# An attention and feed-forward layer in float32: LayerNorm outputs transposed whole, and split into high and low parts behind their transposing

## The chip, the cores and the metric

The kernel runs on one core of a Trainium2 chip. The metric is device time in microseconds (us) for one execution. Three runs of the kernel before took 1685.82, 1691.28 and 1694.91 us; the time before is their median, 1691.28 us.

The engines are called by their short names: PE is TensorE (matrix products and transposes, results in PSUM), PEld its weight loads, DVE is VectorE, ACT is ScalarE, POOL is GpSimd, and SP is the engine from whose queue all DMAs are issued here.

## The reference

`x` has 8 sequences of 1024 tokens with 256 features, in float32.

```python
x = x + layernorm(attn(layernorm(x), Wq, Wk, Wv, Wo))   # eps 1e-5, no weights
x = x + layernorm(ffn(layernorm(x), W, alpha, bias))

# attn: 16 query heads, 4 key/value heads, 16 features a head
q, k, v = x @ Wq, x @ Wk, x @ Wv
q, k = rope(q), rope(k)                     # pairs of neighbouring features
p = softmax(q @ k.T / sqrt(256))            # over all 1024 keys of the sequence
o = (p @ v) @ Wo

# ffn: weights of -1, 0 and 1
delta = 0.7 * mean(abs(W))
out = x @ (where(W > delta, 1, where(W < -delta, -1, 0)) * alpha).T + bias
```

## The kernel before

**Units and steps.** The work goes in 16 units of 512 query tokens (four tiles of 128); two units make a sequence. The inner work of a unit is cut into 32 steps, one for each pair of a head number j (0 to 3, taken for the four key/value heads r together) and a tile of 128 keys; there are 512 steps in all. In a step PE computes the scores with the keys on the partitions (four products, L624, each into a bank of PSUM called "se"), ACT takes their exps (L632, four of 128x512), and PE multiplies the exps of the step before with V (four products, L645, into a bank called "av"). The softmax needs each row's maximum ahead of the exp, so the scores are computed a second time with the queries on the partitions (L569, into pairs of banks called "sm"), DVE takes the maxima (L577), and this pass runs 11 steps ahead of the exps. The maxima of a block of eight steps are combined and split by DVE (L585, L590), transposed, copied by ACT (L598) and written by a DMA (`q_st<-mh`, L605) into two rows of the queries' operand. After the eighth key tile of a head ACT copies the product with V out of its bank (L658), and a DMA sends it to DRAM (`d_av<-avsb`, L666).

**High and low parts.** Products of float32 accuracy are made from operands of the type float32r, split into a high part of 12 significant bits and a low part, the rest. `split_hi` is a cast (L157 on POOL, L159 on ACT), and `split_lo` a subtraction (L162). `product` (L283) sums high by high, high by low and low by high, over two chunks of 128 features: six products for each output, or four where the right operand, the ternary weights, has no low part.

**Projections.** `Project` turns x of a unit into q, k and v. For each half of 256 tokens, `begin` computes LayerNorm's statistics on DVE and POOL (L237 to L243), the normed x on POOL (`xn`, L253), and its two parts on POOL (`xs`, L157 and L162). `x(p, l)` is `transposed` of half p and part l: four transposes of 128x128 against a float32r identity into one "se" bank (L267) and one cast by ACT (L271). Then come the products for k and v together (`kv`), for q (`q_product`), q's rotation on POOL (`rotate`, L297 to L299) and its split (tile `hlq`), and the writing of q and k to DRAM (`q_to_dram`, L471; `kt`, L429 and L480) and back, stacked (L541). The tiles `xs` and `hlq` share one buffer of the tag "hl", but for units 1 and 2, whose `xs` lie in buffers of the exps.

**Tails.** `Tail` is what follows a unit's attention. `fetch` reads the product with V and the softmax's denominators back from DRAM (L696, L701), `invert` and L713 spread the reciprocals, `scale` multiplies and splits on POOL (L719, L157, L162), `attn` is the product with Wo (tile `pa`), `stats_a` the LayerNorm and first sum, `stats_x` the statistics, the normed x and its split, `x(p, l)` the four transposes and the cast (tiles `pt_ot`, `ot`), `ffn` the product with the ternary weights (tile `pf`; L779 on ACT, L780 on POOL), and `stats_f` the last LayerNorm, the sum and the store (L790). The last unit has its own class, `LastTail`, which works by single tiles, transposes both parts at once (`o`), and uses DVE beside POOL.

**What sets the order.** The queues of PE, DVE and ACT are written out by hand over the whole kernel: each step lists its score products, and then the parts that are due in it. The parts' steps stand in tables, in steps from the start of the unit four before for projections (`P_PARTS`, L896), and from the start of the next unit for tails (`T_PARTS`, L907); so every middle unit's 32 steps carry one tail and, from two projections' tables, one projection. The first unit that goes this way has its own steps (`P_FIRST`), and so have the tail of unit 14 (`T_LAST`) and that of unit 15 (`L_PARTS`). Units 0 to 2 are projected in a prologue and ten first steps, -10 to -1, which are listed one by one (L934 to L960). POOL's queue is written by hand up to step 1 and again behind step 512. Between them the order on POOL, and on SP everywhere, is that of a scheduler which places each instruction in an idle place of its engine.

**Buffers.** The maxima use two pairs of banks, the exps' scores three banks, and the product with V one. Every part that needs PSUM takes one of the three "se" banks within its step:

```python
184        if spare[0]:
185            spare[0] += 1
186            if spare[0] % 5 < 2:
187                return ps_mx.tile(shape, dtype, tag="sm", name=name)
188        return ps_e.tile(shape, dtype, tag="se", name=name)
```

(`spare` is nonzero ahead of the first steps and behind the last only.) Work tiles such as `xt`, `ot` and the rotation's `t2` have two buffers each.

Of the kernel before, what the change touches and what calls it, by code (L numbers as in the profile page):

```python
# [28 lines left out]
def kernel(  # L29
# [39 lines left out]
    SPU = G * NK  # steps in a unit  # L69
    NSTEP = NU * SPU  # L70
    LEAD, START = 11, 10  # steps by which the maxima run ahead, and do so at the start
# [24 lines left out]
    # ---- constants and weights  # L96
# [35 lines left out]
    # Operands with parts that never change: rows of -1 in k, of 0 in q, columns of ones in v.  # L132
# [7 lines left out]
    def fill_rows(st, value, lo, n):  # L140
        """Rows lo .. lo + n of each half."""
# [22 lines left out]
    def split(eng, hi, lo, src, hi_eng=None):  # L164
        """src in two parts of 12 significant bits."""
        split_hi(hi_eng or eng, hi, src)
        split_lo(eng, lo, src, hi)

    # Weights in parts.  The columns of w_q go by their place in a pair.
# [9 lines left out]
    # A bank of PSUM for all that is not scores or their product with v.  Before and after those,  # L179
    # the banks of the maxima serve as well.  # L180
# [9 lines left out]
    # Ternary weights, transposed: wt[d, o] = (w[o, d] > delta) - (w[o, d] < -delta)  # L190
# [4 lines left out]
    def measure():  # L195
        ffn["ones"] = work.tile([P, P], F32, tag="qt", name="ones")
# [33 lines left out]
    # ---- layernorm over the last axis of [P, 2, D]  # L230
    def ln_stats(src):
        """(mean, -mean, 1 / sqrt(var + eps)) of each tile."""
# [29 lines left out]
    def transposed(src, tag, name, copy=nc.scalar.copy):  # L262
        """[P, 2, D] -> [P, ND, 2 * P], features on the partitions."""
# [10 lines left out]
    TERMS = ((0, 0), (0, 1), (1, 0))  # parts of the operands in a product  # L274
# [4 lines left out]
    def product(out, left, right, terms=TERMS):  # L279
        """The sum of left[i][:, c]^T right[j][:, c]."""  # L280
# [13 lines left out]
    def rotate(eng, x, cos, sin, t2):  # L294
        """x of [P, 2, n], the two of a pair on the same partition, in place."""
# [5 lines left out]
    # ---- projections of a unit: q and k rotated, transposed and split, v.  q comes out transposed,  # L301
    # with the two columns of a pair on the same partition.
    dq = {}

    class Project:
        """Its parts, each with at most one use of PSUM.  k's pairs are rotated with tokens on the
        partitions in the first units, and in the others by a way over DRAM."""

        def __init__(self, u, eng):
# [4 lines left out]
            if u not in (1, 2):  # L314
                xn = qkp.tile([P, UT, D], F32, tag="xn", name=f"xn_{u}", bufs=2)
                xs = qkp.tile([P, 2, UT, D], F32R, tag="hl", name=f"xs_{u}")
# [17 lines left out]
        def hi(self, p, eng=None):  # L334
            split_hi(eng or self.eng, self.xs[p][:, 0], self.xn[p])
# [692 lines left out]
    with tc.manual_schedule(engines={E.PE, E.DVE, E.Activation, E.Pool}):  # L1028
# [10 lines left out]
        for p in range(2):  # L1039
            p0.norm(p)  # L1040
            p0.hi(p)
# [114 lines left out]
```

## Time and profile before

| | |
|---|---|
| median of three runs | 1691.28 us |
| the profiled execution, its span | 1693.0 us |
| PE busy | 1572.8 us, 93%, 10200 instructions |
| PEld busy | 712.9 us, 42% |
| DVE busy | 1404.3 us, 83% |
| ACT busy | 1254.2 us, 74% |
| POOL busy | 834.1 us, 49% |
| DMA | 117.38 MB, 69 GB/s in the mean |
| granted clock of PE, mean | 0.988 |

The profile shows one execution; its own time is its span, 1693.0 us, which is 1.7 us above the median. Busy times of PE overlap, since its products are pipelined. Each line of the trace names the line of the code, the engine, the operation, and the tile that is written and those that are read, without their numbers: `ot<-pt_ot` is any copy of a transposed half of a tail. In a timeline the first figure is the start in us from the start of the span and the second the length; `x4` means four such instructions in a row, of which the length is the sum or stretch. A bracket such as `[0.69 <-PE sm L569]` tells how long the engine was idle before, and which instruction ended that. The order of the steps is seen from the products with V (L645): the distance from the first of one step to the first of the next is the length of a step.

### The profile page before, as it was taken

How to read it: one execution, taken by the hardware profiler on the slowest of the kernel's cores; microseconds unless marked ns; L12 is line 12 of the kernel's file. 1: busy time of each engine (PE TensorE's matmuls, PEld its weight loads, DVE VectorE, ACT ScalarE, POOL GpSimd, SP SyncE). 2: the span in 40 equal slices, each digit the busy share in tenths (PEclk: the TensorE clock that was granted, in tenths of full speed). 3: DMA queues.
4: the chain of work that ended last, by engine and by line, in shares of the span. 5: the costliest groups of instructions: out<-in, count | busy, mean ns of one | idle time of the engine just before them, and what ended most of it. 6: DMA issues, size and time to landing. Idle time of an engine off the chain costs nothing.

```text
span 1693.0 us, 27812 instructions
## 1 busy us (share of the span) xinstructions
PE 1572.8 (93%) x10200; PEld 712.9 (42%) x10200; DVE 1404.3 (83%) x1815; ACT 1254.2 (74%) x2457; POOL 834.1 (49%) x1239
## 2 busy tenths in 40 slices
PE   7989989999999999999999999999999999999998
PEld 5534343443434444443443434444443443333344
DVE  7877778888898888978888898888888888888884
ACT  4667767777777777777777777777777777777775
POOL 5543364473734637454473735637464362333354
PEclk8999999999999999999999999999999999999999
DMA  4341424134251412514133251412414132141100
GB/s 135 71 90 30 97 68 101 46 79 85 65 96 52 85 58 79 98 48 97 58 73 79 72 101 44 92 53 72 86 53 92 46 79 61 32 85 33 41 14 26
DMA packets 86040, 117.38 MB, mean 69 GB/s; under 512 B 12088, under 2 KB 50808, under 8 KB 85752
## 3 DMA queue, kind: packets, MB, share of 16 engines
q1 hardware_dynamic: 85904, 115.60, 29.7%
q8 instruction: 81, 1.33, 0.3%
q14 instruction: 55, 0.45, 0.1%
HBM read 68.65 MB, written 45.88 MB: 68 GB/s over the span
## 4 chain that ended last, share of the span: by engine, by line
PE 52%; DVE 18%; POOL 10%; ACT 10%; issue 6%; DMA 3%; SPq 1%; POOLq 0%; DVEq 0%; ACTq 0%
PE av L645 19%; PE se L624 17%; DVE mx L577 13%; ACT e L632 9%; PE sm L569 3%; PE pa L283 3%; PE pf L283 2%; PE pq L283 2%; PE pt_xt L267 2%; POOL hl L162 1%; PE pt_ot L267 1%; PE pkv L283 1%; DVE bnst L237 1%; DVE mhl L589 1%; POOL t L297 1%
## 5 line engine op out<-in xcount | busy, mean ns | idle before, releaser
L577 DVE TENSOR_REDUCE mx<-sm 128x2 f32<-128x1024 f32 x1024 | 1199.6, 1217 | 246.2 <-PE se L624 176.4
L632 ACT ACTIVATE e<-se 128x512 f32<-128x512 f32 x2004 | 1045.7, 605 | 315.0 <-PE sm L569 286.8
L624 PE MATMUL se<-q_st,k_st 64*128 64x512 f32 x2048 | 739.4, 445 | 77.7 <-ACT e L632 53.6
L569 PE MATMUL sm<-k_st,q_st 64*128 64x512 f32 x2048 | 758.3, 460 | 12.0 <-DVE mx L577 10.8
L624 PEld LDWEIGHTS se<-q_st,k_st 64*128 64x128 f32 x2048 | 338.5, 185 | 699.1 <-ACT e L632 432.6
L645 PE MATMUL av<-e,v_aug 128*32 128x512 f32 x4096 | 548.1, 606 | 0.0
L569 PEld LDWEIGHTS sm<-k_st,q_st 64*128 64x128 f32 x2048 | 327.2, 185 | 59.1 <-DVE mx L577 42.5
L241 POOL TENSOR_SCALAR lnsc<-mv 128x2 f32<-128x2 f32 (+1 forms) x134 | 26.1, 194 | 432.6 <-DVE mv L239 427.6
L645 PEld LDWEIGHTS av<-e,v_aug 128*32 128x32 f32 x4096 | 80.8, 108 | 87.7 <-issue 53.6
L780 POOL TENSOR_TENSOR a<-a,bias_bc 128x512 f32<-128x512 f32 x30 | 38.4, 1280 | 144.7 <-ACT a L779 144.7
L719 POOL TENSOR_TENSOR xn<-xn,a 128x512 f32<-128x512 f32 x30 | 38.4, 1280 | 122.7 <-DMA a<-d_rec 114.4
L242 POOL TENSOR_TENSOR lnsc<-lnsc,mhalf 128x2 f32<-128x2 f32 (+1 forms) x134 | 92.2, 688 | 0.9
L162 POOL TENSOR_TENSOR hl<-xn,hl 128x512 fp32r<-128x512 f32 x60 | 76.4, 1284 | 0.5
L253 POOL TENSOR_SCALAR xn<-x,lnsc 128x256 f32<-128x256 f32 x116 | 64.8, 566 | 3.5
L283 PE MATMUL pa<-woh,hl 128*128 128x256 f32 x240 | 47.3, 296 | 2.6 <-POOL hl L162 1.2
L237 DVE BATCH_NORM_STATS2 bnst<-a 128x6 f32<-128x256 f32 x120 | 44.5, 413 | 4.1 <-POOL a L780 4.1
L297 POOL TENSOR_TENSOR t<-q_rot,sin_q_sb 128x512 f32<-128x512 f32 x31 | 39.7, 1280 | 14.5 <-ACT q_rot L438 14.3
L283 PE MATMUL pq<-xt,wqkvh 128*128 128x256 f32 x256 | 45.9, 303 | 0.2 <-ACT e L632 0.2
L237 DVE BATCH_NORM_STATS2 bnst<-x 128x6 f32<-128x256 f32 x124 | 46.0, 413 | 0.2 <-DMA x<-in_L_attn_x 0.2
L271 ACT CAST xt<-pt_xt 128x512 fp32r<-128x512 f32 x64 | 39.1, 617 | 4.4 <-PE pt_xt L267 4.4
L271 ACT CAST ot<-pt_ot 128x512 fp32r<-128x512 f32 x66 | 40.7, 618 | 1.9 <-PE pt_ot L267 1.9
L162 POOL TENSOR_TENSOR hlq<-q_rot,hlq 128x512 fp32r<-128x512 f32 x31 | 39.7, 1282 | 4.7 <-ACT hlq L159 4.5
(155 smaller groups left out, 1273.9 us busy)
## 6 DMA issues: line engine op xcount, KB each, us to landing
q_st<-dq SPq DMA_DIRECT2D x90, 256.0 KB
dq<-hlq SPq DMA_DIRECT2D x60, 256.0 KB
d_av<-avsb SPq DMA_DIRECT2D x60, 256.0 KB
x<-in_L_attn_x SPq DMA_DIRECT2D x15, 512.0 KB
xn<-d_av SPq DMA_DIRECT2D x30, 256.0 KB
a<-d_rec SPq DMA_DIRECT2D x30, 256.0 KB
xr<-in_L_attn_x SPq DMA_DIRECT2D x15, 512.0 KB
out_x<-a SPq DMA_DIRECT2D x30, 256.0 KB
```

The costliest lines, as they stand in the source:

```text
L162: eng.tensor_tensor(lo, src, hi.bitcast(F32), ALU.subtract)
L237: nc.vector.bn_stats(st[:, t, :], src[:, t, :])
L242: nc.gpsimd.tensor_tensor(sc[:, 1, :], sc[:, 1, :], mhalf[:, :n], ALU.pow)
L253: eng.tensor_scalar(dst[:, t, :], src[:, t, :], sc[:, 0, t : t + 1] if eng is nc.gpsimd else mv[:, t, 0:1], sc[:, 1, t : t + 1], ALU.add i ...
L271: copy(dst, pt.bitcast(F32))
L283: nc.tensor.matmul(out, chunk(left[i], c), chunk(right[j], c), start=(k == 0), stop=(k == len(steps) - 1),)
L297: eng.tensor_tensor(dst, x, table.unsqueeze(1).to_broadcast(list(x.shape)), ALU.mult)
L569: nc.tensor.matmul(sc[:, a, :], queries[rows], ks[rows, r2, ch * 512 : (ch + 1) * 512], start=True, stop=True,)
L577: nc.vector.tensor_reduce(mx[i][:, ch, t, :, r2], sc, AX.X, ALU.max)
L624: nc.tensor.matmul(sc if len(queries.shape) == 2 else sc.rearrange("p (j t) -> p j t", j=G), ks[rows, r2, kt * P : (kt + 1) * P], queries[ ...
L632: nc.scalar.activation(e[:, a, :], sc, AF.Exp, scale=1.0 / D**0.5)
L645: nc.tensor.matmul(av_ps[0][32 * r : 32 * r + 32, :], va[:, kt, r, :], e[r // 2][:, r % 2, :], start=(kt == 0), stop=(kt == NK - 1),)
```

## The change

LayerNorm's output, which is the left operand of the projections and of ffn, was split into its two parts with tokens on the partitions, and each part was transposed. Now it is transposed once per half, in float32 against the float32 identity `ident`, and split behind that. The new function `transposed_split` does it in one of two ways. With `nc.vector`, ACT casts the high part out of PSUM and DVE subtracts it from the bank for the low part. With `nc.gpsimd`, ACT copies the whole bank to SBUF, into a tile of its own (tag "xt" or "ot", one buffer), and POOL casts and subtracts from there. The projections of units 2 to 15 and the tails of units 0 to 14 go the second way, the projections of units 0 and 1 the first (unit 0's engine is DVE, and unit 1 is given it). The tail of unit 15 stays as it was, with its split in a `stats_x` of its own.

`begin` and the tails' `stats_x` end with the normed x. The tiles `xs` are gone, so the tag "hl" of the projections holds `hlq` alone. `x` becomes one part per half where it was two. In `P_PARTS`, x of half 0 is at step 33 (33 and 34 before), that of half 1 at 43 (43 and 45). In `T_PARTS`, x of half 0 is at step 24 (24 and 25), that of half 1 at 28 (27 and 29). `P_FIRST`, `T_LAST`, the prologue and the first steps lose the same parts and are otherwise hardly moved. The tiles `t2` of q's rotation and those of the tag "qt" get one buffer where they had two. The diff also takes out comments and docstrings, by which lines behind L274 have other numbers; that is left out here.

```diff
@@ transposed() stays; behind it
+    def transposed_split(src, tag, name, lo_eng):
+        pt = psum([P, ND, 2 * P], f"pt_{name}")
+        for t in range(2):
+            for c in range(ND):
+                nc.tensor.transpose(
+                    pt[:, c, t * P : (t + 1) * P], src[:, t, c * P : (c + 1) * P], ident
+                )
+        hi, lo = (
+            work.tile([P, ND, 2 * P], F32R, tag=f"{tag}{l}", name=f"{name}_{l}") for l in range(2)
+        )
+        if lo_eng is nc.vector:
+            split_hi(nc.scalar, hi, pt)
+            split_lo(nc.vector, lo, pt, hi)
+        else:
+            whole = work.tile([P, ND, 2 * P], F32, tag=tag, name=name, bufs=1)
+            nc.scalar.copy(whole, pt)
+            split(lo_eng, hi, lo, whole)
+        return hi, lo
@@ class Project
-                xs = qkp.tile([P, 2, UT, D], F32R, tag="hl", name=f"xs_{u}")
-                self.xs = [xs[:, :, 2 * p : 2 * p + 2, :] for p in range(2)]
-                self.xs = [
-                    ep.tile([P, 2, 2, D], F32R, tag="e", name=f"xs_{u}_{p}") for p in range(2)
-                ]
-        def hi(self, p, eng=None):
-            split_hi(eng or self.eng, self.xs[p][:, 0], self.xn[p])
-        def lo(self, p, eng=None):
-            split_lo(eng or self.eng, self.xs[p][:, 1], self.xn[p], self.xs[p][:, 0])
         def begin(self, p):
             self.stats(p)
             self.norm(p)
-            self.hi(p)
-            self.lo(p)
-        def x(self, p, l):
-            self.xt[p, l] = transposed(self.xs[p][:, l], f"xt{l}", f"xt{l}_{self.u}_{p}")
+        def x(self, p, lo_eng=None):
+            self.xt[p, 0], self.xt[p, 1] = transposed_split(
+                self.xn[p], "xt", f"xt_{self.u}_{p}", lo_eng or self.eng
+            )
...
-            t2 = work.tile([P, 2, 2 * P], F32, tag="t2", name=f"t2_{self.u}_{p}")
+            t2 = work.tile([P, 2, 2 * P], F32, tag="t2", name=f"t2_{self.u}_{p}", bufs=1)
@@ class Tail
-        def x(self, p, l):
-            self.xt[p, l] = transposed(self.hl[p][:, l], f"ot{l}", f"ot{l}_{self.u}_{p}")
+        def x(self, p):
+            self.xt[p, 0], self.xt[p, 1] = transposed_split(
+                self.on[p], "ot", f"ot_{self.u}_{p}", nc.gpsimd
+            )
         def stats_x(self, p):
             self.sc[p] = ln_stats(self.x1[p])
             self.norm(p)
-            self.split(p)
@@ class LastTail
+        def stats_x(self, p):
+            super().stats_x(p)
+            self.split(p)
@@ the tables
     P_PARTS = (
-        (26, "begin", 0), (33, "x", 0, 0), (34, "x", 0, 1), (37, "begin", 1), (43, "x", 1, 0),
-        (45, "x", 1, 1), (49, "kv_and_dram"), (51, "q", 0), (52, "kt"), (53, "v"), (55, "q", 1),
+        (26, "begin", 0), (33, "x", 0), (37, "begin", 1), (43, "x", 1), (49, "kv_and_dram"), (51, "q", 0), (52, "kt"), (53, "v"), (55, "q", 1),
         (57, "q_to_dram"),
...
     T_PARTS = (
...
-        (23, "stats_x", 1), (24, "x", 0, 0), (25, "x", 0, 1), (26, "ffn", 0), (27, "x", 1, 0),
-        (29, "x", 1, 1), (31, "ffn", 1), (31, "stats_f", 0), (33, "stats_f", 1),
+        (23, "stats_x", 1), (24, "x", 0), (26, "ffn", 0), (28, "x", 1), (31, "ffn", 1), (31, "stats_f", 0), (33, "stats_f", 1),
...
-    P_FIRST = (47, 51, 52, 54, 57, 58, 59, 60, 62, 61, 63, 64)
-    T_LAST = (1, 3, 4, 5, 9, 10, 11, 14, 17, 20, 21, 21, 22, 24, 25, 26, 23, 27)
+    P_FIRST = (47, 51, 54, 57, 59, 60, 62, 61, 63, 64)
+    T_LAST = (1, 3, 4, 5, 9, 10, 11, 14, 17, 20, 21, 22, 24, 26, 23, 27)
@@ the first ten steps
-        [second("x", 1, 0), second("x", 1, 1), second("kv", 0)],
+        [second("x", 1, nc.vector), second("kv", 0)],
...
-        [second("q_product", 1), third("stats", 1), third("hi", 0, nc.scalar), third("lo", 0),
-         (pick, "q", 2, 0)],
-        [(pick, "q", 2, 1), third("norm", 1, nc.scalar), third("hi", 1, nc.scalar),
-         third("lo", 1), (keep_warm, 3), (fill_constant_parts, 1)],
-        [third("x", 0, 0), (pick, "q", 3, 0), (keep_warm, 3)],
-        [third("x", 0, 1), (pick, "q", 3, 1), second("rotate_q", 0), (keep_warm, 2)],
-        [third("x", 1, 0), third("x", 1, 1), second("split_q", 0)],
+        [second("q_product", 1), third("stats", 1), (pick, "q", 2, 0)],
+        [(pick, "q", 2, 1), third("norm", 1, nc.scalar), (keep_warm, 3), (fill_constant_parts, 1)],
+        [third("x", 0), (pick, "q", 3, 0), (keep_warm, 3)],
+        [(pick, "q", 3, 1), second("rotate_q", 0), (keep_warm, 2)],
+        [third("x", 1), second("split_q", 0)],
@@ the prologue
             p0.norm(p)
-            p0.hi(p)
-        for p in range(2):
-            p0.lo(p)
...
-        for p in x_parts:
-            part(projects, 0, *p)
+        for p in range(2):
+            p0.x(p)
...
-        p1.hi(0)
-        p1.lo(0)
...
-        p1.hi(1, nc.scalar)
...
-        p1.lo(1, nc.vector)
...
-        p1.x(0, 0)
-        p1.x(0, 1)
+        p1.x(0, nc.vector)
```

More of the change, by code (lines that the diff above doesn't have):

```diff
@@ L195, in measure @@
     def measure():
-        ffn["ones"] = work.tile([P, P], F32, tag="qt", name="ones")
+        ffn["ones"] = work.tile([P, P], F32, tag="qt", name="ones", bufs=1)
         nc.gpsimd.memset(ffn["ones"], 1.0)
@@ L828, in n @@
             if self.eng(t) is nc.gpsimd:
-                po = work.tile([P, G, HKV, 32], F32, tag="qt", name=f"pos_{self.u}_{t}")
+                po = work.tile([P, G, HKV, 32], F32, tag="qt", name=f"pos_{self.u}_{t}", bufs=1)
                 nc.scalar.copy(po, pt)
@@ L921, in keep_warm @@
             nc.tensor.matmul(warm[0], ident_r, sels[0][:, 0, 0], start=True, stop=True)
-    x_parts = [("x", p, l) for p in range(2) for l in range(2)]
     def pick(name, *args):
```

## The prediction

> **What bounds the kernel now.** I read the page first, then the groups by form, then the timeline of one unit of the middle (unit 7, about 785 to 886 us), since the averages mix stages.
>
> ```profile
> span 1693.0 us, 27812 instructions
> PE 1572.8 (93%) x10200; PEld 712.9 (42%) x10200; DVE 1404.3 (83%) x1815; ACT 1254.2 (74%) x2457; POOL 834.1 (49%) x1239
> ```
> TensorE (PE) looks like the bound, but its busy time overlaps itself. What decides is how long one of the 512 steps lasts. I read this off the timeline as the distance between the first L645 products of two steps. In unit 7: a step with no part 2.6 us, with only the copy of a finished block of attention (L658) 2.7, with one x part (four transposes into a score bank, one ACT copy) 3.2, with ffn 3.8, with attn, q or kv 4.3. These figures repeat within 0.1 in units 2 to 12, and such a unit lasts 101.1 us; units 13 and 14, which hold no projection, last 94. So a part costs what it adds to its step. This is why an x part costs 0.6 (timeline of PE and of ACT, step 27 of unit 7; columns: start, length):
>
> ```profile
> 868.78 0.50 PE L624 MATMUL se<-q_st,k_st 64*128 64x512 f32 x1
> ...
> 870.55 0.51 PE L267 MATMUL pt_ot<-ident_r,hl 128*128 128x128 f32 x4
> ...
> 871.99 0.50 PE L624 MATMUL se<-q_st,k_st 64*128 64x512 f32 x1
> ```
> ```profile
> 869.32 2.06 ACT L632 ACTIVATE e<-se 128x512 f32<-128x512 f32 x4 [0.69 <-PE sm L569]
> 871.25 0.62 ACT L271 CAST ot<-pt_ot 128x512 fp32r<-128x512 f32 x1
> 872.52 2.06 ACT L632 ACTIVATE e<-se 128x512 f32<-128x512 f32 x4 [0.66 <-PE sm L569]
> ```
> The next step's first score (871.99) starts when the copy has left its bank (871.87): four exps and one copy in series on ACT, not PE's work, set the step. In the chain of waits L283, L645 and L624 carry PE's 52%, and the list of waits has "se <- ACT ot" 47 times and "xt" 40 times at 0.8 us.
>
> **The change, part by part.** Steps are numbered within a unit; "x(p)" is the transposing of half p.
>
> *Half of the x parts go.* Each half had a high and a low part; it has one now. Of the 4 x parts that leave a middle unit, those of steps 2, 13, 25 and one of 27/29 go: 3.2 to 2.6, 3.1 to 2.6, 3.2 to 2.7 (L658 stays there), 3.2 to 2.6: -0.6 -0.5 -0.5 -0.6 = -2.2 us. Unit 13, without projections, shows the first two steps at 2.6 already.
>
> *The remaining transposes are float32.* L225 does four such:
>
> ```profile
> 136.37 0.66 PE L225 MATMUL pt_w<-ident,up 128*128 128x128 f32 x4 [0.25 <-ACT e L632]
> ```
> against 0.51 above, and the four of L823 take 0.60. So +0.09 to +0.15 an x part, but the transposes end about 0.2 us before ACT is free to copy (871.06 against 871.25), and a float32 copy out of PSUM takes 586 ns (L746) where the cast takes 618. I take 0 of bounds -0.03 and +0.12 for 56 parts (-2 to +7 us).
>
> The Trainium skill, FP8 and Floating Point Precision, TensorE Precision Notes, speaks against this: "True FP32: 4 passes through PE array". By it four transposes would take 4 x 0.51 = 2.0 us, 1.5 more for each of 56, and the kernel would be about 84 us slower. The L225 row has one matmul record to a transpose and 0.66 us, so I go by the row.
>
> *POOL's split moves behind the transposes.* It costs the same (hi 0.62, lo 1.28), but PE's products now wait for it. Three of the four have room: xt(0) at step 1 and xt(1) at 11 are read at 17, ot(1) at 28 is read at 31. ot(0) at 24 is read by ffn(0) at 26, and POOL's queue there is full (POOL's timeline, same unit):
>
> ```profile
> 858.50 1.27 POOL L297 TENSOR_TENSOR t<-q_rot,sin_q_sb 128x512 f32<-128x512 f32 x1
> ...
> 862.88 0.73 POOL L299 TENSOR_TENSOR q_rot<-q_rot,t 128x256 f32<-128x256 f32 x1
> 863.60 1.09 POOL L253 TENSOR_SCALAR xn<-x,lnsc 128x256 f32<-128x256 f32 x2
> ```
> In the built program POOL's order behind L299 is: ot(0) hi, xn(1), hlq hi, ot(0) lo, hlq lo. The rotation starts 0.1 earlier (POOL no longer splits before it, q_rot arrives at 858.31), so lo ends at 863.50 + 0.59 + 1.06 + 0.58 + 1.28 = 867.0. PE came to ffn(0) at 866.65; with step 25 shorter by 0.5 it comes at 866.1, does the two high products (0.25) and stands for 0.7 us. Queued behind it on PE: the rest of ffn, the step's L645, the next scores; DVE and ACT follow. So +0.7 in units 1 to 12, of bounds 0.3 (POOL slightly earlier) and 1.9 (POOL's whole queue to hlq lo).
>
> *attn(0) has no slack.* At step 12 it waits for POOL's scaled attention, which waits for a chain of DMAs begun at step 1. The sixth product of L283 starts 0.05 to 0.5 us after POOL's last lo in units 2 to 12 (0.28 in the mean; where the slack was used up, the 12 products span 2.1 to 2.4 instead of 1.67). Step 2 is 0.6 shorter and the chain is not: +0.3, of bounds 0 and 0.6.
>
> *A collision goes.* At step 28 POOL splits the next unit's xs while DVE splits the maxima:
>
> ```profile
> 875.18 0.59 DVE L585 TENSOR_TENSOR mc<-mx 128x16 f32<-128x16 f32 x1
> 875.80 0.18 DVE L589 CAST mhl<-mc 128x16 fp32r<-128x16 f32 x1
> 876.02 1.14 DVE L590 TENSOR_TENSOR mhl<-mc,mhl 128x16 fp32r<-128x16 f32 x1
> ```
> These two take 250 and 317 ns in the mean; here they end with POOL's L157 and L162. Step 30 then lasts 3.2 (2.8 in units 12 to 14, where no xs is split then). The split leaves step 28: -0.4. The one of xt(1) meets the maxima of step 12 instead, where DVE idles while PE does attn(0): 0, of bounds 0 and +0.4.
>
> The Trainium skill, SBUF — State Buffer, "SBUF: two separate sides", calls the port pair of the two engines an exclusive lock, held for the whole instruction, which the rows bear out.
>
> A middle unit: -2.2 + 0.7 + 0.3 - 0.4 = -1.6; eleven of them (2 to 12, less the 0.4 in 12): **-17.2 us**. Units 13 and 14 lose two x parts each with POOL idle: **-2.2**.
>
> *Start (to step 8 of unit 0).* Unit 0's low halves now stand on DVE behind the statistics of unit 1, whose x lands at 11.6; these end at 13.4, so PE's q product waits for 14.5 instead of starting at 12.3. Unit 1 saves transposes. The load of wo goes into the buffer of xn_2_1, read by transposes at step -1 (62 to 63) and no longer by POOL's split (55.0); POOL's L157 of wo stood at 68.2 waiting for it. SP's issues of dq, dk, k_st and then q_st<-mh (89.8) hang on POOL, and PE's step 8 on that. **+2**, of bounds 0.5 and 4.
>
> *Unit 1.* hlq_3 shared a buffer with xs_4, so POOL waited, and SP's queue, in which a q_st<-mh stands behind dq<-hlq, with it:
>
> ```profile
> 212.30 1.20 POOL L157 TENSOR_SCALAR hlq<-q_rot 128x512 fp32r<-128x512 f32 x2 [7.91 <-PE pt_xt L267]
> ```
> Steps 16 and 17 lasted 5.8 and 5.9 instead of 2.6 and 4.3: -4.8. But dq_3's four DMAs (1 MB) now go out at about 175.6, ahead of d_av:
>
> ```profile
> 173.26 2.31 SPq L541 DMA_DIRECT2D q_st<-dq  x5
> 175.67 0.38 SPq L666 DMA_DIRECT2D d_av<-avsb  x1
> ...
> 186.82 0.64 SPq L696 DMA_DIRECT2D xn<-d_av  x1
> 187.51 0.62 SPq L701 DMA_DIRECT2D den<-d_av  x1
> 188.23 1.42 SPq L605 DMA_DIRECT2D q_st<-mh  x2
> ```
> SP waits at L696 for d_av to land, and PE's step 8 (already 3.7 long through this) for the q_st<-mh behind. The queue moves 0.13 MB/us there, dq alone 0.16: +8 if all is added, +3.3 if the engines' spare half is used; I take **+5**. With three x parts of unit 0/1's own outside the stalls (steps 20 and 26 of unit 0, 13 of unit 1) and unit 1's steps 25 to 30 and ffn(0): -1.6 - 1.1 - 0.4 + 0.7 = -2.4. Unit 1 and the rest of unit 0: -4.8 + 5 - 2.4 = **-2.2**.
>
> *Unit 15.* x(0) at step 21 is read at 22 already. POOL's order is hi, xn(1), lo from 1643.9, so lo ends at 1646.9 where ffn(0) ended at 1645.8: +2, less 0.6 for the x part of step 25: **+1.4**, of 0 and 3.
>
> Sum: -17.2 - 2.2 + 2 - 2.2 + 1.4 = -18.2 us on the profiled span of 1693.0. That span lies 1.7 (0.1%) above the median of the three runs, 1691.28 (1685.82 to 1694.91); on the median it gives **1673 us**, 1.1% faster. A measurement tells this kernel from itself to about 0.5%, 8.5 us.
>
> **The rivals.** (1) *The wait at ffn(0) takes it all: slower.* Place: PE's L283 at step 26, behind POOL's ot lo. Each us is 12 us of the total, and it decides at 0.7 + 18.2 / 12 = 2.2 us: above this the change loses. It needs POOL 1.5 later than worked out; the L241 of the statistics, which stands between the sine and the cosine product, waits for DVE's mv (858.35, used at 859.85, 1.5 early), and that is what speaks against it. At a wait of 3.2: 1703. (2) *Little left.* The wait runs to 1.9 (+14.4) or the start and dq_3 take their upper bounds (+2, +3): 1688. For it: POOL has no gap from 854.85 to 868.36; against: its order is fixed and ot lo is not last. (3) *More gain.* The waits at ffn(0) and attn(0) vanish (-12) and dq_3's traffic is hidden (-5): 1656. Against: slack of 0.05 to 0.5 in ten units. (4) *Hidden anyway*, PE being 93% busy: 1691. Against it unit 13, whose steps 2 and 13 last 2.6.
>
> **How the numbers follow.** Forecast 0.64, its own range 1664 to 1682; (3) 0.12; (2) 0.11 and (4) 0.03, both within 0.5%; (1) 0.10. Faster 0.76, same 0.14, slower 0.10. The unknown costs add to -12 (attn 0.3 x 11, dq_3 1.7, ffn 0.4 x 12, start 1.5, end 1.4) and +18 (ffn 1.2 x 12, start 2, end 1.6): 1661 to 1691, which leaves out (1) and about half of (3).
>
> **What would show it.** Middle units of 99.5 us; steps 2, 13, 25, 27 at 2.6 or 2.7; a gap of about 0.7 within the eight products of L283 for pf(0) put down to POOL's lo; L283's pa(0) spanning 2.0 more often; step 30 at 2.8; unit 1's step 16 at 2.6 and its step 8 near 10. Wrong if x steps keep 3.2, if the float32 transposes outlast ACT's exps, or if PE waits over 2 us at ffn(0).

## The result, and the profile after

The changed kernel takes 1690.07 us (median of 12 runs, 1682.55 to 1694.36), the kernel before 1691.57 us in the 12 runs beside them. The ratio is 0.9992 with a 95% interval of 0.9977 to 1.0006: no difference that can be told, where 1.1% faster was forecast.

The first lines of the page of the changed kernel:

```profile
span 1689.4 us, 27228 instructions
PE 1564.0 (93%) x9952; PEld 697.7 (41%) x9952; DVE 1418.7 (84%) x1816; ACT 1223.6 (72%) x2390; POOL 832.8 (49%) x1239
```

PE has 248 instructions less and ACT 67, as the change says; DVE is busy 14 us longer with one instruction more: the three small instructions that combine and split the maxima (L594 to L599) take 73.7 us, where the same three (L585 to L590) took 58.2. The span is 3.6 us shorter than before. Line numbers have moved: the scores with keys on the partitions are L633, the exps L641, the product with V L654, the maxima L586, their split L594 to L599, the products of `product` L303, the new transposes L279, the whole copy L290.

Read as before, by the distance between the first products with V of two steps, the two profiles give where the time went (us; a negative figure is a gain):

| stretch | predicted | measured |
|---|---|---|
| start, to step 9 of unit 0 | +2 | +0.9 |
| rest of unit 0, and unit 1 | -2.2 | -1.8 |
| units 2 to 12 | -17.2 | -8.1 |
| units 13 and 14 | -2.2 | -1.0 |
| unit 15 | +1.4 | +6.4 |
| sum | -18.2 | -3.6 |

The steps of a middle unit, as means over units 2 to 12 (steps that differ by less than 0.05 are left out):

| step | 1 | 2 | 11 | 12 | 13 | 24 | 25 | 26 | 27 | 28 | 29 | 30 | 31 | unit |
|---|---|---|---|---|---|---|---|---|---|---|---|---|---|---|
| before | 3.19 | 3.19 | 3.19 | 4.50 | 3.13 | 3.19 | 3.19 | 3.80 | 3.20 | 2.61 | 3.19 | 3.22 | 3.81 | 101.16 |
| after | 3.25 | 2.61 | 3.32 | 4.75 | 2.61 | 3.35 | 2.65 | 4.33 | 2.61 | 3.25 | 2.60 | 3.48 | 3.87 | 100.43 |

Steps 2, 13, 25 and 27 lost what was forecast, 2.2 us together, and the part of step 29 is at 28 now. Step 26 holds the wait for POOL's low part. Its views, POOL's and PE's timeline of unit 7, and the same products on PE before the change:

```profile
853.09 1.28 POOL L317 TENSOR_TENSOR t<-q_rot,sin_q_sb 128x512 f32<-128x512 f32 x1 [1.61 <-ACT q_rot L447]
...
858.19 0.61 POOL L157 TENSOR_SCALAR ot<-ot 128x512 fp32r<-128x512 f32 x1
858.80 1.08 POOL L253 TENSOR_SCALAR xn<-x,lnsc 128x256 f32<-128x256 f32 x2
859.86 0.61 POOL L157 TENSOR_SCALAR hlq<-q_rot 128x512 fp32r<-128x512 f32 x1
860.44 1.27 POOL L162 TENSOR_TENSOR ot<-ot,ot 128x512 fp32r<-128x512 f32 x1
```
```profile
861.05 0.48 PE L303 MATMUL pf<-wt,ot 128*128 128x256 f32 x2
861.76 0.97 PE L303 MATMUL pf<-wt,ot 128*128 128x256 f32 x6 [0.24 <-POOL ot L162]
```
```profile
866.65 1.21 PE L283 MATMUL pf<-wt,ot 128*128 128x256 f32 x8
```

POOL's low part ends at 861.71, 8.62 us after its rotation starts; the sum in the prediction was 8.6. PE does the two high products and stands until then. The idle time is only 0.24 us, but the eight products stretch over 1.68 us where they took 1.21.

Step 30 was to fall from 3.2 to 2.8 and rose to 3.48. DVE's timeline of unit 7, and POOL's at the same time:

```profile
869.46 0.61 DVE L594 TENSOR_TENSOR mc<-mx 128x16 f32<-128x16 f32 x1
870.10 0.18 DVE L598 CAST mhl<-mc 128x16 fp32r<-128x16 f32 x1
870.32 1.15 DVE L599 TENSOR_TENSOR mhl<-mc,mhl 128x16 fp32r<-128x16 f32 x1
```
```profile
869.43 0.62 POOL L157 TENSOR_SCALAR ot<-ot 128x512 fp32r<-128x512 f32 x1 [2.15 <-ACT ot L290]
870.13 1.29 POOL L162 TENSOR_TENSOR ot<-ot,ot 128x512 fp32r<-128x512 f32 x1
```

DVE's two small instructions last 0.61 and 1.15 us and end with POOL's cast and subtraction, just as before. Only the tile on POOL is another: `ot`, the tail's second half, in place of `xs`. And units 13 and 14, where nothing was split at this place before, have step 30 at 3.48 too, where it was 2.84.

In unit 15 the tail of unit 14 has its first product with the ternary weights at step 22. PE's and POOL's timelines there:

```profile
1634.66 0.51 PE L303 MATMUL pf<-wt,ot 128*128 128x256 f32 x2
1637.13 0.97 PE L303 MATMUL pf<-wt,ot 128*128 128x256 f32 x6 [1.96 <-POOL ot L162]
```
```profile
1633.88 0.73 POOL L157 TENSOR_SCALAR ot<-ot 128x512 fp32r<-128x512 f32 x1
1634.60 1.25 POOL L253 TENSOR_SCALAR xn<-x,lnsc 128x256 f32<-128x256 f32 x2
1635.82 1.25 POOL L162 TENSOR_TENSOR ot<-ot,ot 128x512 fp32r<-128x512 f32 x1
...
1646.53 0.62 POOL L157 TENSOR_SCALAR ot<-ot 128x512 fp32r<-128x512 f32 x1
1647.23 0.19 POOL L241 TENSOR_SCALAR lnsc<-mv 128x1 f32<-128x1 f32 x1
1647.50 0.19 POOL L243 TENSOR_SCALAR lnsc<-mv 128x1 f32<-128x1 f32 x1
1647.65 1.28 POOL L162 TENSOR_TENSOR ot<-ot,ot 128x512 fp32r<-128x512 f32 x1
```

The first wait is 1.96 us, and steps 22 and 23 are 3.9 us longer together (6.25 and 3.91 for 3.34 and 2.87). Not all of this is the wait: behind it the granted clock was 0.50 from about 1638 to 1641.5. In the run below that moves the first product with the ternary weights in the other units, and leaves this tail as it is, the same wait was 1.97 us, the clock stayed at 1.00, and steps 22 and 23 took 5.78 and 2.85. The next products with V behind the wait, first of the changed kernel, then of that run with its wait:

```profile
1639.18 1.93 PE L654 MATMUL av<-e,v_aug 128*32 128x512 f32 x8
```
```profile
1631.59 0.97 PE L303 MATMUL pf<-wt,ot 128*128 128x256 f32 x6 [1.97 <-POOL ot L162]
...
1633.22 1.06 PE L654 MATMUL av<-e,v_aug 128*32 128x512 f32 x8
```

So the wait is worth 2.4 us here and the clock behind it 1.5. The second half's split stands at 1646.5 to 1648.9 between the statistics of the last tail (`128x1`), and steps 29 to 31 are 3.1 us longer together (11.8 for 8.7), with the clock at 0.50 from 1662.0 to 1668.8.

### The profile page after: what moved, and what is told of

Its sections match the earlier page's. It is cut to its first block, busy times and chain, and to the rows that moved or that the text cites. A ratio compares the mean times of both kernels' runs of the same rounds, so it can differ in the third digit from the quotient of the medians.

```text
span 1689.4 us, 27228 instructions
## 1 busy us (share of the span) xinstructions
PE 1564.0 (93%) x9952; PEld 697.7 (41%) x9952; DVE 1418.7 (84%) x1816; ACT 1223.6 (72%) x2390; POOL 832.8 (49%) x1239
## 4 chain that ended last, share of the span: by engine, by line
PE 53%; DVE 19%; ACT 10%; POOL 9%; DMA 5%; issue 3%; SPq 1%; POOLq 0%; DVEq 0%; ACTq 0%
PE av L654 20%; PE se L633 18%; DVE mx L586 14%; ACT e L641 10%; PE sm L578 4%; PE pq L303 3%; PE pa L303 3%; PE pf L303 2%; DMA a<-d_rec 1%; PE pkv L303 1%; DVE mhl L599 1%; DVE bnst L237 1%; POOL hl L162 1%; POOL q_rot L317 1%; POOL t L317 1%
## 5 line engine op out<-in xcount | busy, mean ns | idle before, releaser
L586 DVE TENSOR_REDUCE mx<-sm 128x2 f32<-128x1024 f32 x1024 | 1199.4, 1217 | 211.3 <-PE se L633 158.7
L641 ACT ACTIVATE e<-se 128x512 f32<-128x512 f32 x2004 | 1047.0, 603 | 322.9 <-PE sm L578 283.7
L633 PE MATMUL se<-q_st,k_st 64*128 64x512 f32 x2048 | 737.1, 444 | 78.0 <-ACT e L641 44.4
L578 PE MATMUL sm<-k_st,q_st 64*128 64x512 f32 x2048 | 759.1, 462 | 13.9 <-DVE mx L586 12.3
L633 PEld LDWEIGHTS se<-q_st,k_st 64*128 64x128 f32 x2048 | 337.5, 185 | 695.3 <-ACT e L641 460.6
L654 PE MATMUL av<-e,v_aug 128*32 128x512 f32 x4096 | 548.9, 608 | 0.1
L654 PEld LDWEIGHTS av<-e,v_aug 128*32 128x32 f32 x4096 | 81.1, 108 | 102.9 <-issue 70.6
L303 PE MATMUL pa<-woh,hl 128*128 128x256 f32 x240 | 47.8, 296 | 4.9 <-POOL hl L162 3.6
L303 PE MATMUL pq<-xt,wqkvh 128*128 128x256 f32 x256 | 46.0, 303 | 3.1 <-DVE xt L162 2.7
L303 PE MATMUL pf<-wt,ot 128*128 128x256 f32 x256 | 42.0, 298 | 6.8 <-POOL ot L162 4.6
L303 PEld LDWEIGHTS pq<-xt,wqkvh 128*128 128x128 f32 x256 | 36.2, 196 | 12.8 <-ACT e L641 8.8
L303 PEld LDWEIGHTS pa<-woh,hl 128*128 128x128 f32 x240 | 35.1, 189 | 15.1 <-POOL hl L162 5.8
```

Of the source, the lines that this page charges most:

```text
L303: nc.tensor.matmul(out, chunk(left[i], c), chunk(right[j], c), start=(k == 0), stop=(k == len(steps) - 1),)
L578: nc.tensor.matmul(sc[:, a, :], queries[rows], ks[rows, r2, ch * 512 : (ch + 1) * 512], start=True, stop=True,)
L586: nc.vector.tensor_reduce(mx[i][:, ch, t, :, r2], sc, AX.X, ALU.max)
L633: nc.tensor.matmul(sc if len(queries.shape) == 2 else sc.rearrange("p (j t) -> p j t", j=G), ks[rows, r2, kt * P : (kt + 1) * P], queries[ ...
L641: nc.scalar.activation(e[:, a, :], sc, AF.Exp, scale=1.0 / D**0.5)
L654: nc.tensor.matmul(av_ps[0][32 * r : 32 * r + 32, :], va[:, kt, r, :], e[r // 2][:, r % 2, :], start=(kt == 0), stop=(kt == NK - 1),)
```

## The experiments

All are edits of the changed kernel, but for the last. Where one profile alone was taken, its span stands against 1689.4 us of the changed kernel and 1693.0 us of the kernel before. The 12 runs of the changed kernel have spans of 1680.6 to 1692.3 us, so one span alone shows little, and the differences are read by steps; most repeat within 0.1 us from unit to unit, step 12 does not.

**The collision taken away, nothing moved.** The low part of the second half is left out, and the high part stands in its place.

```diff
         if lo_eng is nc.vector:
...
+        elif lo_eng is None:
+            split_hi(nc.scalar, hi, pt)
+            lo = hi
...
             self.xt[p, 0], self.xt[p, 1] = transposed_split(
-                self.on[p], "ot", f"ot_{self.u}_{p}", nc.gpsimd
+                self.on[p], "ot", f"ot_{self.u}_{p}", nc.gpsimd if p == 0 else None
             )
```

> Left out: the split of the second half of each tail's transposed LayerNorm output; ACT casts the high part straight out of PSUM and the product with the ternary weights uses it twice. PE and ACT have the same instructions in the same steps as in the changed kernel, only POOL's cast and subtraction behind step 28 are gone. Theory A (this split keeps POOL and DVE from each other while DVE splits the maxima): step 30 of units 2 to 14 falls from 3.48 to 2.84 us, DVE's subtraction L599 at step 29 from 1.15 to about 0.3, all other steps stay; 13 x 0.64 = 8.3 us less than the 1689.4 us of the changed kernel's profile, 1681. Theory B (step 30 is long because the transposes and the copy of step 28 push the maxima's products back): step 30 stays at 3.48, the time at 1689.

Step 30 was 2.83 in units 2 to 12, and 2.83 in 13 and 14; steps 28 and 29 stayed at 3.25 and 2.61. DVE's three small instructions took 0.18, 0.18 and 0.19 us in unit 7. The span is 1681.9, 7.5 us less. Theory A holds: with the same work on PE and ACT, the step's length hangs on POOL's split alone. Unit 15 falls from 99.7 to 96.3, all of it in steps 29 to 31 (8.4 for 11.8), so the split of the second half is also what lengthens the end.

**The second half's transposes one step later.**

```diff
-        (23, "stats_x", 1), (24, "x", 0), (26, "ffn", 0), (28, "x", 1), (31, "ffn", 1), (31, "stats_f", 0), (33, "stats_f", 1),
+        (23, "stats_x", 1), (24, "x", 0), (26, "ffn", 0), (29, "x", 1), (31, "ffn", 1), (31, "stats_f", 0), (33, "stats_f", 1),
```

> The changed kernel with one number changed: the second half's transposes of a tail at step 29 where they were at 28. Theory A (POOL's split meets DVE's split of the maxima at step 28 to 29): the split now comes behind it, step 28 goes from 3.25 to 2.6, step 29 from 2.6 to 3.25, step 30 from 3.48 to 2.84: 13 x 0.64 = 8.3 us less than the changed kernel, 0.5%. Theory B (it is the place of the transposes, not the split): the long step moves to step 31 and nothing is gained. A third way: the split now ends too late for the product with the ternary weights at step 31, which gives back up to 0.6 us a unit.

Steps 28, 29 and 30 were 2.61, 3.25 and 2.83, step 31 stayed at 3.87. The median is 1683.23 us, the ratio to the kernel before 0.9938 (0.9923 to 0.9953). DVE's timeline of unit 7 in this kernel:

```profile
867.37 0.18 DVE L594 TENSOR_TENSOR mc<-mx 128x16 f32<-128x16 f32 x1
867.58 0.18 DVE L598 CAST mhl<-mc 128x16 fp32r<-128x16 f32 x1
867.80 0.19 DVE L599 TENSOR_TENSOR mhl<-mc,mhl 128x16 fp32r<-128x16 f32 x1
```

The same three instructions end 0.62 us after the first began, against 2.01 us above. Theory A again, and the third way (too late for step 31) does not show.

**The first product with the ternary weights one step later.**

```diff
-        (23, "stats_x", 1), (24, "x", 0), (26, "ffn", 0), (28, "x", 1), (31, "ffn", 1), (31, "stats_f", 0), (33, "stats_f", 1),
+        (23, "stats_x", 1), (24, "x", 0), (27, "ffn", 0), (28, "x", 1), (31, "ffn", 1), (31, "stats_f", 0), (33, "stats_f", 1),
```

> The changed kernel with one number changed: the first product with the ternary weights of a tail at step 27 where it was at 26. If PE waits there for POOL's low part, the wait is gone: steps 26 and 27 together from 4.33 + 2.61 to 2.6 + 3.85, so 0.45 us a unit less in units 2 to 12 and nothing in 13 and 14: 1689.4 - 5 = 1684. The rival: POOL's addition of the bias behind this product (1.27 us) moves into the time in which DVE splits the maxima, and step 30 grows from 3.48 by up to 0.6, which takes it all: 1689 or more.

Steps 26 and 27 were 2.61 and 3.87, 0.46 less together; step 30 stayed at 3.48. The wait is gone and nothing took its place. The span is 1682.3; the wait explains 5 us of the 7, and unit 15, which the edit doesn't touch, was 1.8 shorter in this run, most of it behind the wait at step 22, where the clock stayed at 1.00.

**Only the projections' half of the change.** `Tail.x`, the tails' `stats_x` and the tails' steps are those of before.

> Only the projections' half of the change; the tails split and transpose as before, at the steps of before. If the tails' half costs what it gains and more: a middle unit of before (101.16) less 0.58 and 0.53 (steps 2 and 13), plus 0.18 (float32 transposes, steps 1 and 11), less 0.38 (no POOL split while DVE splits the maxima: step 30 from 3.22 to 2.84), plus 0.25 (attention's first product) = 100.1; units 13 to 15 as before (94.2, 94.2, 93.4); start and unit 1 as in the changed kernel (0.9 less). In all 1693.0 - 0.9 - 11 x 1.06 = 1680 on the profile, 0.75% faster than before. The rival, that both halves gain alike: half of the changed kernel's gain, 1691.

The median is 1685.14 us, the ratio 0.9942 (0.9924 to 0.9960). Middle units last 100.30 in the mean (100.1 was expected), with step 30 at 2.83; units 13 to 15 last 94.7, 93.9 and 93.3, as before. Half the change is faster than the whole, so the tails' half cost more than it gained. The profile's span, 1684.5, is 4.5 us above the expectation: step 8 of unit 1 took 13.7 us here, and step 12 of unit 2 took 6.4, both waits for DMAs.

**The tail of unit 14 split by ACT and DVE.**

```diff
             self.xt[p, 0], self.xt[p, 1] = transposed_split(
-                self.on[p], "ot", f"ot_{self.u}_{p}", nc.gpsimd
+                self.on[p], "ot", f"ot_{self.u}_{p}", nc.vector if self.u == NU - 2 else nc.gpsimd
             )
```

> The changed kernel, but the tail of unit 14, which runs in unit 15, splits the first way: ACT casts the high part out of PSUM and DVE subtracts from the bank. Theory A (unit 15 is longer because PE waits for POOL's low part at step 22, and because POOL's split of the second half stands ahead of the statistics of the last tail): steps 22 and 23 go from 6.25 and 3.91 to about 3.4 and 2.9, steps 29 to 31 from 11.8 together to about 8.7, and unit 15 from 99.7 to 93 to 94, as before the change. 1689.4 - 6 = 1683. Rival B (only the wait at step 22 is the split's doing): unit 15 at 96. Rival C: DVE, which has the last maxima until step 21 and half of the last tail, is the new bound, and unit 15 stays above 97.

Steps 22 and 23 were 3.3 and 2.9, steps 29 to 31 were 8.8 together, and unit 15 lasted 92.7, with a span of 1683.2: theory A. PE's timeline at step 22 has the eight products in one row:

```profile
1635.03 1.18 PE L303 MATMUL pf<-wt,ot 128*128 128x256 f32 x8
```

**Unit 3's queries to DRAM later, twice.** The first try moved one number of `P_FIRST`:

```diff
-    P_FIRST = (47, 51, 54, 57, 59, 60, 62, 61, 63, 64)
+    P_FIRST = (47, 51, 54, 57, 59, 60, 62, 61, 63, 74)
```

> The changed kernel with one number changed: unit 3's queries are written to DRAM ten steps later (step 10 of unit 1 where it was step 0). Theory A (this 1 MB of traffic ahead of the attention's output in SP's queue is what step 8 of unit 1 waits for): step 8 falls from 10.8 us to 3 or 4.9 at most, no other step grows, 6 to 8 us less: 1682. Rival B (step 8 waits for the attention's output for another reason): it stays at 10 to 11 and the time at 1689. Rival C: the traffic now hits the reciprocals' way over DRAM, and step 12 of unit 1 grows by as much as step 8 falls.

In the changed kernel the four DMAs of unit 3's queries (`dq<-hlq`) stand ahead of the sending of attention's output (`d_av`), of its reading (`xn<-d_av`) and of the maxima's rows (`q_st<-mh`), which step 8 waits for:

```profile
177.36 2.67 SPq L480 DMA_DIRECT2D dq<-hlq  x4
181.50 0.34 SPq L675 DMA_DIRECT2D d_av<-avsb  x1
...
193.03 0.64 SPq L705 DMA_DIRECT2D xn<-d_av  x1
...
194.44 1.41 SPq L614 DMA_DIRECT2D q_st<-mh  x2
```
```profile
197.87 0.76 PE L633 MATMUL se<-q_st,k_st 64*128 64x512 f32 x1 [7.60 <-DMA q_st<-mh]
```

With the edit, step 8 of unit 1 stayed at 10.5. This decided nothing, because the scheduler put two of the four DMAs at 178.8 us, still ahead of the reading of attention's output, and two ahead of the maxima's rows. So the second try moved what these DMAs read as well:

```diff
-    P_FIRST = (47, 51, 54, 57, 59, 60, 62, 61, 63, 64)
+    P_FIRST = (47, 51, 54, 57, 59, 60, 62, 61, 73, 74)
```

> The changed kernel with two numbers changed: unit 3's second half of q, and its queries' way to DRAM, at steps 9 and 10 of unit 1 where they were at the end of unit 0. In the run before this one (queries to DRAM ten steps later) half of that traffic still went out ahead of the attention's output and the other half ahead of the maxima, so it decided nothing; here all of it stands behind the maxima's rows that step 8 waits for, as before the change. Theory A (that traffic is what step 8 waits for): step 8 of unit 1 falls from 10.8 us to about 4.9, 5 to 6 us less than the changed kernel: 1684. Rival B (the wait has another cause in the start): it stays above 9, 1689. Rival C: the traffic hits the reciprocals' way over DRAM, and step 12 of unit 1 grows by as much.

Now step 8 is 7.2 and step 9 5.1. Step 9 holds 1.7 us of the product that came from step 31 of unit 0 (2.6 there for 4.3). So the two steps lose 14.0 - (12.3 - 1.7) = 3.3 us of the 5.0 that the change had added to them (8.9 before). The second of the two versions with all moves (below) has the same move, and there they lose 14.0 - (14.1 - 1.7) = 1.5. Without this 1.7 they take 10.6 and 12.4, less than in any run that leaves the traffic in its place (13.0 to 16.9). The last run, of the kernel before, shows it from the other side: its edit frees the buffer that unit 3's queries had to wait for, their four DMAs go out at 177.49, steps 16 and 17 of unit 1 fall to 2.6 and 4.3, and steps 8 and 9 take 13.3. So this traffic is a cause; its share is not settled by two executions that differ so. SP issues the maxima's rows at 187.43 here, and PE goes on with the next scores at 194.63, 7.2 us later (8.2 in that version); before the change it was 4.3 us (188.23 and 192.50). What else delays these 16 KB wasn't tried. SP's and PE's timeline of this run:

```profile
187.43 1.42 SPq L614 DMA_DIRECT2D q_st<-mh  x2
```
```profile
194.63 0.54 PE L633 MATMUL se<-q_st,k_st 64*128 64x512 f32 x1 [4.19 <-DMA q_st<-mh]
```

The span of this run is no shorter (1693.2), since step 12 lasted 5.7 in unit 8 and 7.9 in unit 9. That step is the next experiment.

**Attention's first product one step later.**

```diff
-        (1, "fetch"), (7, "invert"), (8, "scale", 0), (9, "scale", 1), (12, "attn", 0),
+        (1, "fetch"), (7, "invert"), (8, "scale", 0), (9, "scale", 1), (13, "attn", 0),
```

> The changed kernel with one number changed: attention's first product of a tail at step 13 for 12, a step that the change has emptied. Theory A (this product has no slack against the chain of DMAs and POOL's scaling that began at step 1): step 12 falls to 2.6 in every unit, step 13 is 4.35 in every unit, together 6.96 for 7.36 in the mean of units 2 to 12, and the single units with 5 us and more at step 12 are gone: 14 x 0.4 = 5.6 us less, 1684. Rival B (POOL is the later one and simply comes later still): step 13 is 4.8 in the mean and nothing is gained, 1689.

Step 12 is 2.61 and step 13 is 4.35, each within 0.1 in all of units 1 to 14; in the changed kernel step 12 ran from 4.3 to 5.4. Theory A; the span is 1681.2. This wait was 0.40 us a unit in the mean, of which the change had added 0.25 by these two profiles; the other runs with this product at step 12 have 4.6 to 5.0 there in the mean, where the kernel before has 4.5.

**The same transposes in float32r.** The tiles of the normed x get the type float32r as well.

```diff
-        pt = psum([P, ND, 2 * P], f"pt_{name}")
+        pt = psum([P, ND, 2 * P], f"pt_{name}", F32R)
...
-                    pt[:, c, t * P : (t + 1) * P], src[:, t, c * P : (c + 1) * P], ident
+                    pt[:, c, t * P : (t + 1) * P], src[:, t, c * P : (c + 1) * P], ident_r
```

> Left out: the low half of the normed x. It is written as float32r, so that the same transposes run in float32r against the float32r identity, as before the change; copy, cast and subtraction follow as in the changed kernel. Theory A (the float32 transposes cost 0.06 to 0.16 us a part): steps 1, 11, 24 and 28 of a middle unit go from 3.25, 3.32, 3.35 and 3.25 to 3.19 or below, 0.4 us a unit, 4.5 us in all: 1685. Rival B (the kind of the transposes is hidden behind ACT's exps, and these steps are longer for POOL's and ACT's order): they stay, 1689.

Steps 1, 11, 24 and 28 are 3.14, 3.19, 3.20 and 3.13, so 0.11 to 0.15 us less each, about 0.5 us a unit: the kind of the transposes is seen, theory A. But the time is not shorter: 1690.1, and a middle unit lasts 100.54. Step 26 is 0.18 longer than in the changed kernel and step 30 0.11, for PE comes earlier to waits whose end has not moved; step 12, which varies from run to run, has 0.25 more. Unit 15 shows what the clock did in the changed kernel: here it stayed at 1.00 through steps 29 to 31, and these took 9.1 us, 0.5 more than before the change. The groups by form, first of the changed kernel, then of this one (busy us, mean ns of one):

```profile
L279 PE MATMUL pt_xt<-ident,xn 128*128 128x128 f32 x128 | 21.7, 297 | 1.2
```
```profile
L279 PE MATMUL pt_xt<-ident_r,xn 128*128 128x128 f32 x128 | 17.3, 260 | 1.6 <-DVE xn L253 0.4
```

**The moves together**, first with the first of the two moves of unit 3's queries, then with the second:

> The changed kernel with five moves together: the second half's transposes of a tail at step 29 for 28, the first product with the ternary weights at 27 for 26, attention's first product at 13 for 12, unit 3's queries to DRAM ten steps later, and the tail of unit 14 split by ACT and DVE. If the causes are those named and do not overlap: 8.3 + 5 + 4 (step 12 from 4.75 to 2.6 and step 13 from 2.6 to 4.3, 14 units) + 7 + 6 = 30 us less than the changed kernel's profile, 1659 us, 2% faster than before. If they hide one another (the rival): 1675.

> The version with all moves, but with the move of unit 3's queries of the run beside it. If step 8 of unit 1 falls from 10.2 to 5: 1661 - 5 = 1656 on the profile, 2.1% faster than the kernel before. If rival B or C holds: 1661.

The medians are 1665.07 us, ratio 0.9829 (0.9811 to 0.9846), and 1662.07 us, ratio 0.9805 (0.9789 to 0.9821). Which of the two is faster isn't told by these. A middle unit lasts 98.9 and 99.0 us, and the units 2 to 12 differ by at most 0.6 where they differed by 1.2. The expected 1659 was nearly reached by the first (span 1660.9); the 7 us expected from its move of the queries did not come, as the run above says, and the other moves gave more than they were put down for (attention's, put down at 4, gives 14 x 0.4 = 5.6 by its own run). In the second, step 8 of unit 1 is 8.4 and not 5.

**The kernel before with two of the moves.** `attn(0)` at step 13, and the first half of `xs` in a buffer of its own; the tiles `t2` and those of the tag "qt" get one buffer, as in the change.

```diff
-        (1, "fetch"), (7, "invert"), (8, "scale", 0), (9, "scale", 1), (12, "attn", 0),
+        (1, "fetch"), (7, "invert"), (8, "scale", 0), (9, "scale", 1), (13, "attn", 0),
...
-                xs = qkp.tile([P, 2, UT, D], F32R, tag="hl", name=f"xs_{u}")
+                xs0 = qkp.tile([P, 2, 2, D], F32R, tag="xs0", name=f"xs0_{u}")
+                xs1 = qkp.tile([P, 2, UT, D], F32R, tag="hl", name=f"xs1_{u}")
...
-                self.xs = [xs[:, :, 2 * p : 2 * p + 2, :] for p in range(2)]
+                self.xs = [xs0, xs1[:, :, :2, :]]
```

> The kernel before the change, with the two moves that can be made in it too: attention's first product at step 13 for 12, and the first half of the parts to be transposed in a buffer of its own, so that POOL's split of it need not wait until the queries are written and comes ahead of DVE's split of the maxima (the rotation's tile gets one buffer to make room). If the collision and the reciprocals' way are causes in that kernel too: step 30 from 3.22 to 2.84, steps 12 and 13 from 7.63 to 6.95, a middle unit from 101.16 to 100.1, in all 13 us less: 1680 on the profile, 0.8% faster. Then what the change itself is worth is seen between this kernel and the version with all moves: about 20 us. If the moves help only the changed kernel: 1690.

The median is 1688.98 us, the ratio 0.9960 (0.9947 to 0.9974). Step 30 is 2.83, as expected: the collision cost the kernel before 0.39 us a unit. Steps 12 and 13 are 2.61 and 4.84, together 7.45 and not 6.95, because step 13 holds an x part in that kernel, so the product has no free step to go to. The change empties that step. With the waits moved away in both, a middle unit lasts 100.56 without the change and 99.0 with it.

## Why the prediction was right or wrong

**How the bound was read: right.** A part costs what it adds to its step. Steps 2, 13, 25 and 27 and the pair 28 and 29 gave -2.18 us a unit where -2.2 stood. The rival that PE's load hides it falls.

**The wait at the first product with the ternary weights: right.** +0.53 where +0.7 stood, and the move to step 27 took 0.46 of it away.

**Attention's first product: right.** +0.25 for +0.3, and the run that moves it shows that there was no slack. That the two agree so closely is in part luck, since the other runs give +0.1 to +0.5.

**"A collision goes. The split leaves step 28: -0.4": wrong, the largest error, and the step that failed.** The split of `xs` left, but the split of `ot(1)`, which the change moved behind its transposes, came to the same place. Its room was checked against its reader on PE (28 to 31), and not against what DVE does at that time. Measured +0.25 in the mean of units 2 to 12 and +0.64 in 13 and 14: 2.8 + 1.3 us lost where 4.0 were to be gained, 8.1 us of the 14.6 that are missing. Taking the split away and moving it both bring step 30 to 2.83.

**Float32 transposes, taken as 0: mis-sized.** The four take 0.66 us, as the row of L225 said, but the 0.15 more is not hidden: +0.06, +0.12 and +0.16 at steps 1, 11 and 24 and 0.06 at 28, 0.4 us a unit, between 4 and 5 us in all. The ground given, that the transposes end 0.2 us before ACT is free, was taken from one step, and the whole copies took 596 ns in the projections and 617 in the tails (medians), not 586. By the Trainium skill's four passes (FP8 and Floating Point Precision, TensorE Precision Notes) it would have been 1.5 us a part; these transposes do not show it.

**Unit 15, +1.4 of 0 to 3: mis-sized, +6.4.** The wait at step 22 was 1.96 us, as worked out (2). By itself it makes step 22 2.4 us longer and step 23 no longer, as three runs with the same tail and the clock at 1.00 show (5.8 and 2.9). The other 1.5 us there came with a granted clock of 0.50 behind the stall, which the prediction had at nothing. And the second half's split on POOL ahead of the last tail's statistics was not looked at: 3.1 us in steps 29 to 31, of which 0.5 are left in the run with float32r transposes, where the clock stayed at 1.00 there. Splitting by ACT and DVE took both away, 7.0 us. The 6.4 is the upper end: five other profiles with the same tail have unit 15 at 97.2 to 98.8 us, 3.9 to 5.4 more than before.

**The start and unit 1: right in size, in part by luck.** +0.9 for +2 and -1.8 for -2.2. Step 16 of unit 1 went to 2.6, step 8 to 10.8 ("near 10"). That unit 3's queries are a cause there is shown, but not how much of it they are. The start of one profile says little: the runs with the same start leave step 9 at 99.2 to 102.6 us, the kernel before at 100.0.

The median lies within the range of 1661 to 1691, but not in the forecast's own, 1664 to 1682, and no rival came true as it was told. The time is that of "little left", but the wait at the first product did not run to 1.9 us; two places that no rival named did it. Two slips in the working change nothing: the lower costs add to 12.7 and not 12, and the three lines said to carry PE's 52% of the chain carry 44.

## What to carry to other kernels

When an instruction of POOL is moved, look at three things at its new time: who reads its result, what else stands in its queue, and what DVE does in the same microsecond. A gain that is credited to a collision that ends needs a look at what the change itself puts into the freed place. Removing parts empties steps; the gain was whole only after the products that waited had been moved into these.

## What the runs showed of the hardware that was not expected

A short stall of PE can cost more than its length, since the granted clock may fall behind it. The table by stretches of the changed kernel at the end of unit 15, 1 us each (after the stretch: its length, busy us and instructions of PE, PEld, DVE, ACT, POOL, then the clock, the DMA share, GB/s):

```profile
1659.00:1660.00 1.00, 0.26 (x2) 0.12 (x2) 1.00 (x1) 0.00 (x0) 1.00 (x1) 1.00 0.00 0
1660.00:1661.00 1.00, 0.62 (x4) 0.41 (x4) 0.54 (x2) 0.00 (x0) 0.04 (x1) 1.00 0.02 7
1661.00:1662.00 1.00, 1.00 (x10) 0.16 (x8) 0.97 (x3) 0.78 (x1) 0.00 (x0) 0.98 0.76 255
1662.00:1663.00 1.00, 1.00 (x7) 0.37 (x3) 0.03 (x1) 0.25 (x1) 0.79 (x3) 0.50 0.00 0
...
1667.00:1668.00 1.00, 1.00 (x8) 0.35 (x10) 0.88 (x3) 0.45 (x1) 0.69 (x2) 0.50 0.00 0
1668.00:1669.00 1.00, 1.00 (x8) 0.18 (x2) 0.28 (x1) 1.00 (x2) 0.00 (x0) 0.60 0.00 0
```

PE was busy for 0.26 and 0.62 us of two stretches, the longest idle time being 1.12 us, and from 1662 on it had half the clock for 6.8 us. The kernel before shows it at step 8 of unit 1, behind a stall of 1.62 us:

```profile
191.00:192.00 1.00, 0.00 (x0) 0.00 (x0) 0.36 (x1) 0.00 (x0) 0.34 (x1) 1.00 0.57 124
192.00:193.00 1.00, 0.50 (x2) 0.53 (x4) 0.55 (x1) 0.00 (x0) 0.00 (x0) 0.59 1.05 372
193.00:194.00 1.00, 1.00 (x8) 0.42 (x5) 0.21 (x1) 0.70 (x2) 0.00 (x0) 0.50 0.29 79
```

Step 9, which falls into this time, lasts 4.1 us, where it takes 2.7 in the units behind. In the run that splits unit 14's tail by ACT and DVE the clock stays at 1.00 through these steps. The Trainium skill, TensorE: Matmul & The Clock Gate, What's actually happening, says that the clock is halved after at least one idle window of about 3.4 us; in these two places idle times of 1.1 to 1.6 us were enough.

They are not always. Behind the wait at step 22 of unit 15 the clock fell to 0.50 in the changed kernel (1.96 us idle) and stayed at 1.00 in the run that moves the first product with the ternary weights (1.97 us idle):

```profile
1639.00:1640.00 1.00, 1.00 (x6) 0.20 (x8) 0.00 (x0) 1.00 (x2) 1.00 (x1) 0.50 0.00 0
```
```profile
1633.00:1634.00 1.00, 1.00 (x10) 0.16 (x8) 0.00 (x0) 1.00 (x3) 0.58 (x1) 1.00 0.00 0
```

So the length of the stall alone does not decide; what does decide was not tried. It makes one profile of the same steps differ from the next by more than a microsecond.

The float32 transposes took 0.66 us for four, against 0.51 in float32r: 1.3 times, not four times.
